# Turning attention keys on VectorE and through DRAM, and a new row order for the layer-norm tiles

## The chip, the core and the metric

The kernel runs on one core of one Trainium2 chip, as one launch. The time is device time in microseconds, from the runs of the whole program. A run with the profiler on gives the trace; its span runs from the first to the last recorded instruction. The engines are called here as the profile calls them: PE (TensorE: matrix products and transposes), DVE (VectorE), ACT (ScalarE), POOL (GpSimd) and SP (SyncE, which here only issues DMAs). Each engine works through its own list of instructions in order and waits on semaphores where an operand is not ready.

## What is computed

The input x is 2 sequences of 1024 tokens with 512 features, in float32. Four blocks follow, each added to its own input:

```
x = x + attn_a(layernorm(x))    # chunked linear attention with decay, 4 heads of 128
x = x + ffn(layernorm(x))       # gated, weights are integer codes with scales, 1408 hidden
x = x + attn_b(layernorm(x))    # softmax attention, one head of 512
x = x + ffn(layernorm(x))       # the same weights again
```

The change is mostly in the first block. For each chunk of 128 tokens and each head it computes

```
k      = k / max(norm(k), 1e-12)
attn   = (q @ k.T) * beta * decay          # causal
y      = attn @ v + (q @ state) * chunk_decay
state  = state * total_decay + v.T @ (k * beta * decay_to_end)
```

The product q @ k.T needs the key with its 128 features across the partitions (its transpose), while the state needs it with the tokens across the partitions. So every key tile is needed in both layouts.

## The kernel before

**Tiles.** Rows of x are cut in 16 tiles of 128 tokens (NT = 16), and these in 4 groups of ST = 4 tiles (NST = 4). Between the blocks x lies in DRAM, one DRAM tile for each row tile (x1, x2, x3, lines 139 to 141). Most products are made in three passes of a high and a low part (`mm3`, line 88), which `split` (line 73) makes: ACT copies the high part, DVE or POOL subtracts it to get the low one.

**Layer norm in groups.** `ln_norm` (line 188) loads a row tile, normalizes it, and turns it on DVE into a staging tile y. DVE turns blocks of 32 by 32 only, so the blocks have still to be put in place: `ln_move` (line 201) does that by DMAs from SBUF to SBUF, four for each of four blocks b, that is 16 of 64 KB for a group. There are 14 such groups in all, with 224 moves: the profile has 152 on SP and 72 on POOL. Row tile i of group st is the 128 rows in a line from row 512 st + 128 i, so a move writes 16 runs of 32 values (128 bytes) on each partition. `ln_split` (line 214) or `combine` (line 242) then make high and low parts. The first two groups of the first block are turned on PE instead (`layernorm_T`, line 125).

**The first attention's loop** (lines 749 to 804) takes one tile in each step t. It emits, in this order: one query head of four steps ahead (`q_head`, line 500: 12 products of 512 columns), the key and value of tile t + 1 (`kv_tile`, line 577), the scores of tile t (`scores`, line 617), every fourth step the gate projection of a coming group (`gate_proj`, line 426), the decay of tile t + 1 (`decay`, line 528), and fillers: layer-norm steps of later groups by the table at line 733, weight codes (`down_weights`, line 304) and, in the last three steps, operands and products of the block that follows. `scores(t)` begins with

```
            pkT = psum(f"pkT{t}").rearrange("p (h c) -> p h c", h=H)
            for h in range(H):
                nc.tensor.transpose(pkT[:, h, :], kf[:, h, :], ident)
            kT = tl("kT", t)
            copied = nc.scalar.copy(kT, pkT).ins
```

(lines 620 to 624): PE turns the key of each of the four heads into PSUM, and ACT copies it to SBUF as kT. Then come the state's products (pd, line 635), the outputs of the tile before (`chunk_out`, line 660: pl, pg), and the scores proper (pS, line 650), which read kT as the stationary operand. DVE weighs pS by decay into the tile at (line 654). The key itself is taken from PSUM to SBUF as sWk by DVE (line 571) one step earlier, in `kv_part` (line 558), and its squared norms are made on ACT (`k_norm`, line 581).

**Order.** The tile framework takes the program's order as priorities, and settles each engine's list before the run by a model of the times; `behind` (line 66) adds an order among instructions of one engine. At the table of line 733 the first four entries of a group are its four `ln_norm` steps, the last four its four `ln_move` steps; the number is the loop step in which each is emitted. Groups 2 and 3 of the first block are split at steps 3 and 7 (line 771), one step before their first query head. Row tiles of x1 are written by `chunk_out(t)`, which `scores(t + 1)` calls.

**What follows.** After the loop comes `spill` (line 177) of a product V to DRAM, by way of tiles that take the place of sq, kT, kw and sdec. `ffn` (line 808) does the gated block with 11 hidden tiles twice, the second attention follows, and `ffn` again. Both call `ln_steps` (line 225) for their layer norms.

## Time and profile before

| what | value |
|---|---|
| median of 3 runs | 927.32 us (926.01 to 927.61) |
| the profiled execution | 926.9 us |
| its span | 925.2 us, granted PE clock 1.00 |
| instructions | 13659 |
| busy: PE, DVE, ACT, POOL | 918.5, 690.4, 433.9, 257.4 us |
| DMA packets | 216182, of these under 512 bytes 151024 |
| DMA bytes | 162.20 MB, mean 175 GB/s |

How to read it: busy time is the time in which an engine had at least one instruction running, so instructions that overlap count once. A group's mean is the length of one instruction, and where instructions are pipelined the distance from start to start is shorter than that. "Idle before" is the time in which an engine stood still ahead of an instruction, with what ended the wait. In rows of slices each digit is a fortieth of the span (23.1 us), in tenths. DMA rows give the size and the median time from issue to landing; SPq is SP's queue of instructions.

The stages of the run, from the lines at work on PE: preparation to 49 us, the first attention's loop to about 231, the first gated block to 455, the second attention (its first products from 442) to 701, the last gated block to the end.

### The profile page before, as it was taken

Reading aid. Unit: us, or ns where it says so; the run is one execution under the profiler, and the core shown is the slowest. Engines: PE = TensorE matmul, PEld = TensorE weight load, DVE = VectorE, ACT = ScalarE, POOL = GpSimd, SP = SyncE. Lnnn points to the kernel's source line nnn. Section 1 sums busy time; section 2 is a strip of 40 time slices with the busy share of each in tenths; the row PEclk is TensorE's granted clock in tenths of the full one; section 3 lists DMA queues with packets and bytes.
Section 4 is the critical chain, followed back from the end, with each engine's and each line's share of the span. In section 5 each row is a group of like instructions: output and inputs, shape, how many; then the busy total and the mean of one; then the engine's idle time right before and its main releaser. Section 6 shows DMA issues by size and latency. Waiting matters only on the chain.

```text
span 925.2 us, 13659 instructions
## 1 busy us (share of the span) xinstructions
PE 918.5 (99%) x4546; PEld 778.1 (84%) x4546; DVE 690.4 (75%) x1335; ACT 433.9 (47%) x928; POOL 257.4 (28%) x458
## 2 busy tenths in 40 slices
PE   9999999999999999999999999999999999999998
PEld 7899999998888888888888888888878888888887
DVE  6755657479998798778848878569968886967654
ACT  5645365556776334444234444145434444344431
POOL 4345334557563002211130401140501631001100
PEclk9999999999999999999999999999999999999999
DMA  9535655477979754724733769225969735454022
GB/s 304 210 100 124 208 160 152 158 207 262 367 236 321 214 178 153 216 47 150 281 82 83 171 168 261 69 45 137 239 140 369 259 126 137 165 205 138 22 69 80
DMA packets 216182, 162.20 MB, mean 175 GB/s; under 512 B 151024, under 2 KB 167728, under 8 KB 216112
## 3 DMA queue, kind: packets, MB, share of 16 engines
q1 hardware_dynamic: 212624, 150.05, 53.7%
q0 software_dynamic: 3488, 11.28, 4.5%
q8 instruction: 36, 0.59, 0.3%
q14 instruction: 34, 0.28, 0.1%
HBM read 104.76 MB, written 41.84 MB: 158 GB/s over the span
## 4 chain that ended last, share of the span: by engine, by line
PE 94%; DVE 2%; SPq 1%; DMA 1%; issue 1%; ACT 0%; POOL 0%; DVEq 0%; ACTq 0%
PE pXf L338 4%; PE pog L925 4%; PE pog L924 4%; PE pZf L338 4%; PE pof L925 4%; PE pXg L338 4%; PE pVg L338 4%; PE pVf L338 4%; PE pZg L338 4%; PE pof L924 4%; PE pob L91 3%; PE pob L89 3%; PE pob L90 3%; PE psZ L1023 2%; PE psX L1023 2%; PE psV L1023 2%
## 5 line engine op out<-in xcount | busy, mean ns | idle before, releaser
L924 PE MATMUL pog<-wdg,hsg 128*128 128x512 f32 (+1 forms) x165 | 60.1, 375 | 0.0
L925 PE MATMUL pog<-wdg,hsg 128*128 128x512 f32 (+1 forms) x165 | 60.0, 375 | 0.0
L925 PE MATMUL pof<-wdf,hsf 128*128 128x512 f32 x154 | 59.1, 389 | 0.0
L924 PE MATMUL pof<-wdf,hsf 128*128 128x512 f32 x154 | 58.9, 389 | 0.0
L91 PE MATMUL pob<-vh,ptl 128*128 128x512 f32 x128 | 49.9, 390 | 0.8 <-DVE ptl L76 0.8
L89 PE MATMUL pob<-vh,pth 128*128 128x512 f32 x128 | 49.9, 390 | 0.0
L90 PE MATMUL pob<-vl,pth 128*128 128x512 f32 x128 | 49.8, 389 | 0.0
L76 POOL TENSOR_TENSOR hsg<-sgg,hsg 128x128 fp32r<-128x128 f32 x40 | 18.9, 491 | 110.4 <-ACT hsg L75 102.6
L338 PE MATMUL pXg<-B_g,wcg 128*128 128x512 f32 x176 | 46.2, 389 | 0.0
L338 PE MATMUL pVf<-T_f,wcf 128*128 128x512 f32 x176 | 46.2, 389 | 0.0
L338 PE MATMUL pVg<-T_g,wcg 128*128 128x512 f32 x176 | 46.2, 389 | 0.0
L338 PE MATMUL pXf<-B_f,wcf 128*128 128x512 f32 x176 | 45.9, 390 | 0.0
L113 POOL TENSOR_SCALAR ve_g<-mv_g 128x1 f32<-128x1 f32 x16 | 7.7, 486 | 129.6 <-DVE mv_g L111 129.6
L209 POOL DMA_DIRECT2D xT_g<-y_g x48 | 31.1, 655 | 38.5 <-DVE T_b L76 29.2
L338 PEld LDWEIGHTS pXf<-B_f,wcf 128*128 128x128 f32 x176 | 32.9, 188 | 7.1 <-issue 0.3
L338 PEld LDWEIGHTS pVf<-T_f,wcf 128*128 128x128 f32 x176 | 33.0, 188 | 6.9
L338 PEld LDWEIGHTS pVg<-T_g,wcg 128*128 128x128 f32 x176 | 33.0, 188 | 6.9
L338 PEld LDWEIGHTS pXg<-B_g,wcg 128*128 128x128 f32 x176 | 33.0, 188 | 6.9
L545 ACT ACTIVATE row<-row,ncl 128x128 f32<-128x128 f32 x64 | 20.5, 391 | 35.4 <-POOL row L534 35.4
L113 POOL TENSOR_SCALAR ve_b<-mv_b 128x1 f32<-128x1 f32 x16 | 5.7, 359 | 112.4 <-DVE mv_b L111 112.2
L924 PEld LDWEIGHTS pog<-wdg,hsg 128*128 128x128 f32 x165 | 31.1, 188 | 5.7
L925 PEld LDWEIGHTS pog<-wdg,hsg 128*128 128x128 f32 x165 | 31.0, 188 | 5.6
(344 smaller groups left out, 2837.4 us busy)
## 6 DMA issues: line engine op xcount, KB each, us to landing
wcg<-wc SPq DMA_DIRECT2D x19, 896.0 KB, 5.0
wc<-wcf SPq DMA_DIRECT2D x11, 896.0 KB, 5.8
p<-py SPq DMA_DIRECT2D x15, 512.0 KB, 3.5
wcf<-wc SPq DMA_DIRECT2D x8, 896.0 KB, 6.3
ptl<-p SPq DMA_DIRECT2D x56, 128.0 KB, 3.1
xin_a<-in_x SPq DMA_DIRECT2D x16, 256.0 KB, 5.3
xra<-in_x SPq DMA_DIRECT2D x16, 256.0 KB, 3.4
row<-cl SPq DMA_DIRECT2D x16, 256.0 KB, 4.3
```

The source lines that it names most:

```text
L76: return c.ins, (eng or nc.vector).tensor_tensor(lo, src, hi.bitcast(F32), ALU.subtract).ins
L89: nc.tensor.matmul(ps, lhs_hi, rhs_hi, start=first, stop=False)
L90: nc.tensor.matmul(ps, lhs_hi, rhs_lo, start=False, stop=False)
L91: end = nc.tensor.matmul(ps, lhs_lo, rhs_hi, start=False, stop=last).ins
L113: nc.gpsimd.tensor_scalar(ve, mv[:, 1:2], EPS, None, ALU.add)
L209: (nc.sync if sync else nc.gpsimd).dma_start(out=xf[32 * b : 32 * (b + 1), :, c, :], in_=y[32 * c : 32 * (c + 1), b].rearrange("p k i q -> ...
L338: nc.tensor.matmul(ps, w[:, m, k * P : (k + 1) * P], o[:, s, k, :], start=first and k == 0 and s == 0, stop=k == 1 and s == 1, skip_group_ ...
L545: nc.scalar.activation(row[:, h, :], row[:, h, :], AF.Exp, bias=ncl[:, n : n + 1], scale=-1.0)
L924: nc.tensor.matmul(ps, hs[i][0][:, j], wd[j][:, ds], start=j == 0, stop=False)
L925: nc.tensor.matmul(ps, hs[i][1][:, j], wd[j][:, ds], start=False, stop=j == KH - 1)
L1023: ends[nm] = nc.tensor.matmul(ps, o[:, i, k], w[:, j, k], start=first and k == 0 and i + j == 0, stop=k == 1 and i == 1, skip_group_check= ...
```

## The change

Three things change.

1. **Keys.** `scores` no longer turns the key on PE. The new function `turn_key`, which `kv_tile` calls between the key and the value of a tile, turns all four heads on DVE in blocks of 32 by 32 (tile ky), writes the result to a DRAM tile k_d (256 KB) and reads it back by four DMAs (64 KB each, in pieces of 128 bytes) to kT, all on SP. `key_copy`, which other steps are put behind, now holds the DVE instruction in place of the ACT copy, and `k_norm` of the next tile is put behind nothing. The tiles sq and ky have one buffer each; sq had two. The V spill uses the buffers of at in place of sq.
2. **Row order in a layer-norm tile.** DRAM tiles of x1, x2 and x3 now hold a whole group (512 rows). Tile i of a group takes 32 rows of each quarter of the group, in place of 128 rows in a line. After DVE's turn a move then writes 4 runs of 128 values (512 bytes) on each partition, in place of 16 runs of 32. The number of moves and their bytes are the same. Since a tile takes rows of all four row tiles, its load waits until all four are written.
3. **Order of the steps.** The table that places the layer-norm steps in the loop of the first attention has new numbers.

The diff, cut to its core (what is left out gives the functions below groups in place of row tiles):

```diff
+    def in_tiles(groups):
+        return [x[i * P : (i + 1) * P, :] for x in groups for i in range(ST)]
+
-    x1 = [dp.tile([P, D], F32, tag=f"x1_{t}", name=f"x1_{t}") for t in range(NT)]
...
+    x1_g = [dp.tile([ST * P, D], F32, tag=f"x1_{g}", name=f"x1_{g}") for g in range(NST)]
+    x1 = in_tiles(x1_g)
...
+    k_d = [dp.tile([P, 4, P], F32, tag=f"k_{t}", name=f"k_{t}") for t in range(NT)]
...
             if (nm, n) not in lnX:
-                lnX[nm, n] = load_x(src[n], f"{nm}{n}")
+                rows = src[st].rearrange("(c i q) d -> i c q d", c=4, i=ST)
+                lnX[nm, n] = load_x(rows[n - st * ST], f"{nm}{n}")
...
-        xf = lnT[nm, st].bitcast(F32).rearrange("p k (i b q) -> p (k i) b q", i=ST, b=4)
+        xf = lnT[nm, st].bitcast(F32)
...
-                out=xf[32 * b : 32 * (b + 1), :, c, :],
-                in_=y[32 * c : 32 * (c + 1), b].rearrange("p k i q -> p (k i) q"),
+                out=xf[32 * b : 32 * (b + 1), :, c * P : (c + 1) * P],
+                in_=y[32 * c : 32 * (c + 1), b].rearrange("p k i q -> p k (i q)"),
...
+        def turn_key(t):
+            y = tl("ky", t, pool=a1)
+            turned = nc.vector.transpose(
+                y.rearrange("p h c -> p (h c)"), kva[t][0].rearrange("p h c -> p (h c)")
+            ).ins
+            key_copy[:] = [turned]
+            nc.sync.dma_start(out=k_d[t], in_=y)
+            kTa[t] = kT = tl("kT", t)
+            placed = k_d[t].rearrange("(c q) h (b j) -> b q h c j", c=4, b=4)
+            for b in range(4):
+                nc.sync.dma_start(
+                    out=kT[32 * b : 32 * (b + 1)].rearrange("p h (c j) -> p h c j", c=4), in_=placed[b]
+                )
+
         def kv_tile(t):
             kv_part(t, "Wk")
+            turn_key(t)
             kv_part(t, "Wv")
...
-            sq = tl("sq", t)
+            sq = tl("sq", t, pool=a1)
...
-            pkT = psum(f"pkT{t}").rearrange("p (h c) -> p h c", h=H)
-            for h in range(H):
-                nc.tensor.transpose(pkT[:, h, :], kf[:, h, :], ident)
-            kT = tl("kT", t)
-            copied = nc.scalar.copy(kT, pkT).ins
-            key_copy[:] = [copied]
+            kT = kTa.pop(t)
             if t == 0:
-                with behind((copied,)):
+                with behind(key_copy):
                     decay(0)
             if t + 1 < NT:
-                k_norm(t + 1, copied)
+                k_norm(t + 1)
...
-            (xa, "a", 2, (0, 0, 0, 1, 1, 1, 1, 1)),
-            (xa, "a", 3, (2, 2, 3, 4, 4, 5, 5, 5)),
-            (x1, "f", 0, (6, 6, 7, 7, 7, 7, 8, 8)),
-            (x1, "f", 1, (9, 9, 10, 10, 10, 10, 11, 11)),
+            (x_g, "a", 2, (0, 0, 0, 1, 1, 1, 2, 2)),
+            (x_g, "a", 3, (3, 3, 4, 4, 5, 5, 6, 6)),
+            (x1_g, "f", 0, (7, 7, 7, 7, 8, 8, 9, 9)),
+            (x1_g, "f", 1, (10, 10, 10, 10, 11, 11, 11, 11)),
...
-        spilled = spill(ap, ("sq", "kT", "kw", "sdec"), next(prep)[0], vo_d, "V")
+        spilled = spill(ap, ("at", "kT", "kw", "sdec"), next(prep)[0], vo_d, "V")
```

More of the change, by code (lines that the diff above doesn't have):

```diff
@@ L136, in hybrid_block_kernel @@
     bq_s, sg_s, su_s = cols[:, 0:H], cols[:, H : H + KH], cols[:, H + KH : H + 2 * KH]
+    def in_tiles(groups):
+        return [x[i * P : (i + 1) * P, :] for x in groups for i in range(ST)]
     x_in = a["x"]
-    x1 = [dp.tile([P, D], F32, tag=f"x1_{t}", name=f"x1_{t}") for t in range(NT)]
-    x2 = [dp.tile([P, D], F32, tag=f"x2_{t}", name=f"x2_{t}") for t in range(NT)]
-    x3 = [dp.tile([P, D], F32, tag=f"x3_{t}", name=f"x3_{t}") for t in range(NT)]
+    x1_g = [dp.tile([ST * P, D], F32, tag=f"x1_{g}", name=f"x1_{g}") for g in range(NST)]
+    x1 = in_tiles(x1_g)
+    x2_g = [dp.tile([ST * P, D], F32, tag=f"x2_{g}", name=f"x2_{g}") for g in range(NST)]
+    x2 = in_tiles(x2_g)
+    x3_g = [dp.tile([ST * P, D], F32, tag=f"x3_{g}", name=f"x3_{g}") for g in range(NST)]
+    x3 = in_tiles(x3_g)
     cl_d = [dp.tile([16, P], F32, tag=f"cl_{g}", name=f"cl_{g}") for g in range(NST)]
+    k_d = [dp.tile([P, 4, P], F32, tag=f"k_{t}", name=f"k_{t}") for t in range(NT)]
     p_d = [dp.tile([T // P, P, P], F32, tag=f"p_{i}", name=f"p_{i}") for i in range(NC)]
@@ L367, in hybrid_block_kernel @@
         normed, key_copy, late_norm = {}, [], []
-        xTa, za, gta, sca, qTa, kva, ata, deca, sta, rowa, facta = ({} for _ in range(11))
+        xTa, za, gta, sca, qTa, kva, ata, deca, sta, rowa, facta, kTa = ({} for _ in range(12))
         wqkv = {}
@@ L410, in load_wqkv @@
             return load if staged is None else done
-        xa = [x_in[t * P : (t + 1) * P, :] for t in range(NT)]
+        x_g = [x_in[g * ST * P : (g + 1) * ST * P, :] for g in range(NST)]
+        xa = in_tiles(x_g)
         def ln_tile(t):
@@ L916, in ffn @@
                     with behind((half,)):
-                        nc.sync.dma_start(out=xr, in_=src[t])
+                        nc.sync.dma_start(out=xr, in_=in_tiles(src)[t])
                     o = fp.tile([P, 512], F32, tag="sg", name=f"o{nm}{t}")
@@ L940, in hybrid_block_kernel @@
     ffn(
-        x1,
+        x1_g,
         x2,
@@ L946, in hybrid_block_kernel @@
         spilled,
-        (ln_steps(x2, "b", 0) + ln_steps(x2, "b", 1), of_b[:6]),
+        (ln_steps(x2_g, "b", 0) + ln_steps(x2_g, "b", 1), of_b[:6]),
     )
@@ L1201, in hybrid_block_kernel @@
         for b in range(NB):
-            nm, src, g = ("b", x2, 2) if b == 0 else ("g", x3, 0)
+            nm, src, g = ("b", x2_g, 2) if b == 0 else ("g", x3_g, 0)
             norm = ln_steps(src, nm, g) + ln_steps(src, nm, g + 1)
@@ L1277, in hybrid_block_kernel @@
     out_t = [out[t * P : (t + 1) * P, :] for t in range(NT)]
-    ffn(x3, out_t, "g", wcs, moving, ended, ([], []))
+    ffn(x3_g, out_t, "g", wcs, moving, ended, ([], []))
 def _layouts(i):
```

## The prediction

> **What bounds the kernel now.** I began with the page's busy shares, its slices and its chain of work.

> ```profile
> PE 918.5 (99%) x4546; PEld 778.1 (84%) x4546; DVE 690.4 (75%) x1335; ACT 433.9 (47%) x928; POOL 257.4 (28%) x458
> ...
> DVE  6755657479998798778848878569968886967654
> ...
> PEclk9999999999999999999999999999999999999999
> ...
> PE 94%; DVE 2%; SPq 1%; DMA 1%; issue 1%; ACT 0%; POOL 0%; DVEq 0%; ACTq 0%
> ```

> PE (TensorE) is busy 918.5 of 925.2 us at the full granted clock, and 94% of the chain is its own work. Whatever leaves PE is gained one for one, unless a wait takes its place. VectorE (DVE) is full in slices 10 to 12 (208 to 278 us). Next I asked for the tile that the change takes away, pkT, and for TensorE in order of time about it.

> ```profile
> L622 PEld LDWEIGHTS pkT<-ident,sWk x64: 138/141/144, 49.2 to 217.6; 128*128 128x128 f32 x64
> L622 PE MATMUL pkT<-ident,sWk x64: 270/273/274, 49.3 to 217.7; 128*128 128x128 f32 x64
> L624 ACT COPY kT<-pkT x16: 562/585/588, 50.0 to 221.0; 128x512 f32<-128x512 f32 x16
> ...
>   PE pS L650: 0.4, 1
> ```

> ```profile
> 49.19 0.28 PE L91 MATMUL pWv<-Wv,xl_a 128*128 128x256 f32 x1
> 49.31 0.60 PE L622 MATMUL pkT<-ident,sWk 128*128 128x128 f32 x4
> 49.75 0.61 PE L635 MATMUL pd<-sWv,kw 128*128 128x128 f32 x4
> ```

> The 273 ns of one transpose overlap the next. What counts is start to start: four take 49.75 - 49.31 = 0.44 us, and the matmul before them takes 0.12 whatever follows. The other tiles show the same step (64.36 to 64.79, 163.57 to 164.01).

> **The keys, on PE and ScalarE.** 16 tiles x 0.44 us leave PE: **-7.0 us**. The single PE wait for this copy goes too (0.40 us ahead of 100.59): **-0.4**. 16 copies of 0.585 us leave ScalarE, which is 56% busy between 49 and 222 us; that shortens nothing on the path.

> **The keys, the new way.** Each tile now takes one VectorE transpose of 128x512, one write of 256 KB on SyncE's queue (SP) and, once that has landed, four reads of 64 KB in pieces of 128 bytes. The nearest rows:

> ```profile
> L198 DVE STREAM_TRANSPOSE y_a<-xn_a x8: 670/711/714, 60.1 to 108.6; 128x512 f32<-128x512 f32 x8
> ```

> ```profile
> x<-xra SPq DMA_DIRECT2D x16, 256.0 KB, 2.3
> ...
> xT_a<-y_a SPq DMA_DIRECT2D x32, 64.0 KB, 2.1
> ```

> ```profile
> L1116 SPq DMA_DIRECT2D ptl<-p x56: 303/600/2538, 502.7 to 675.5; - x56
> ...
> DMA to landing us min/median/max: 2.1/3.1/5.0
> ```

> The first is the same VectorE form; x<-xra has the write's size; ptl<-p, in the second attention, is the same write-then-four-reads pattern at twice the size. From the moment VectorE begins to take the key out of PSUM: 0.68 (that row, L571) + 0.70 + 2.3 + three issues of 0.60 ahead of the last read + 3.1 = **8.6 us**. The reads lie between ptl's 3.1 and xT_a's 2.1; I take the longer.

> The room for it is the time from the start of sWk (L571) to the first pS (L650) of the same tile, less 0.44 for the transposes that go. By the trace, for tiles 0 to 15: 9.3, 18.1, 12.6, 15.0, 15.5, 19.9, 12.0, 13.8, 13.4, 19.1, 14.4, 14.9, 10.5, 12.1, 10.2, 10.6. The key is made a loop step before its scores, so all 16 have room; the shortest margins are 0.7 (tile 0), 1.6 (tile 14), 1.9 (tile 12) and 2.0 us (tile 15). In an in-order queue a late key is paid in full: pS waits on PE, and behind it stand the gate projection or the next query head. Bounds: nothing, and 21.5 us if both legs take their worst (worked out under the rivals). I take **+0.5**, since only tile 0 lies within a microsecond, and other PE work may be planned ahead of it.

> **VectorE.** 16 x 0.70 = 11.2 us are added to an engine that is 64% busy between 49 and 222 us. Its idle time hides that until about 197 us. From there I read it in 8 us stretches (the columns are PE, PEld, VectorE, ScalarE, GpSimd, each busy and count, then clock, DMA share, GB/s):

> ```profile
> 197.00:205.00 8.00, 8.00 (x61) 7.50 (x60) 6.87 (x14) 3.10 (x13) 4.26 (x7) 1.00 0.68 182
> 205.00:213.00 8.00, 8.00 (x61) 7.50 (x60) 6.93 (x14) 6.29 (x14) 5.24 (x7) 1.00 1.04 390
> 213.00:221.00 8.00, 8.00 (x45) 6.86 (x45) 8.00 (x18) 7.17 (x18) 4.31 (x6) 1.00 0.64 217
> 221.00:229.00 8.00, 8.00 (x53) 7.15 (x53) 6.75 (x14) 3.86 (x7) 7.84 (x8) 1.00 0.51 192
> 229.00:237.00 8.00, 8.00 (x37) 6.59 (x36) 7.96 (x15) 4.66 (x8) 4.66 (x8) 1.00 0.89 357
> 237.00:245.00 8.00, 8.00 (x37) 6.64 (x36) 7.42 (x13) 7.07 (x10) 4.87 (x9) 1.00 1.00 333
> ```

> VectorE is busy 43.9 of these 48 us: 4.1 us idle. Two more transposes (tiles 14 and 15) take 1.4 of that, and PE arrives earlier by three sets of transposes, 1.3 us. So 1.4 us stays idle and the cover just holds on average; if none of the idle time can be used, PE waits 2.7 us. Bounds 0 and 2.7; I take **+1.0**, nearer to nothing, because in 213 to 221 VectorE is full and PE still does not wait.

> **SP.** Per tile 0.33 + 4 x 0.60 = 2.7 us of issue are added, and the first read stands behind the landing of its write (2.3 us), with everything later on that queue behind it: the rows of decays (row<-cl), residuals (xra) and layer-norm moves. What waits for those is VectorE and ScalarE, not PE; their cover is the room above and PE's next 8 to 10 us. Loss: inside the 0.5.

> **Layer-norm moves.** Instead of 16 runs of 128 bytes per partition, each of the 224 moves now has 4 of 512. On SP an xT_a move takes 0.63 us and 16 of them 11.9 us (75.42 to 87.33); the write p<-py, which has 512-byte pieces, issues in 0.37 us. So some 0.25 us of SP time per move goes, 16 us over the 64 moves issued in the first attention. No PE instruction waits for a move there, so I cost it at **0** (bounds: -0.4, which is already counted, and +1 if a split comes late).

> [...]

> **Spread and row choice.** The moves of groups 2 and 3 go one or two steps later; they must precede the splits at steps 3 and 7, and the last move now falls in step 2 and step 6. A layer-norm tile now needs four earlier row tiles instead of one, but the first such step (7 for x1 tiles 0 to 3) comes three steps after the last of them is written. The squares get one buffer, and only ScalarE writes them. The V spill takes the "at" buffers, free after L668 at 228.9 us, while the product ends at 231.5. All at 0.

> **Sum.** The profiled execution took 926.9 us (span 925.2): 926.9 - 7.0 - 0.4 + 0.5 + 1.0 = **921.0**. The median of the runs shown is 0.4 above it: **921.4**.

> **Rivals.** *Chance 0.62: the forecast*, 918.5 to 923.5.

> *Chance 0.15: VectorE or the keys take half back.* VectorE's whole 2.7 and a chain of 10.6 us (late by 1.3, 0.1 and 0.4 at tiles 0, 12 and 14): 926.9 - 7.4 + 2.7 + 1.8 = 924.0, or 924.4. For it speaks the full stretch at 213; against it, that PE waits for VectorE only 1.3 us in the whole run.

> *Chance 0.12: no change that shows.* A chain of 11.0 us (1.7, 0.5, 0.8, 0.4 late) and the 2.7: 925.6, or 926.0; also the case that the new order of instructions spoils as much as it frees. A measurement of this kernel tells about 0.2% (1.9 us) from no change.

> *Chance 0.11: slower.* One mechanism: both DRAM legs take as long as these rows at their worst, 5.8 us for the write (the longest x<-xra) and 5.0 for a read, as the first attention's queue is shared with weight and code loads. The chain is then 0.68 + 0.70 + 5.8 + 1.8 + 5.0 = 14.0 us, and tiles 0, 2, 6, 7, 8, 12, 13, 14, 15 are late by 4.7, 1.4, 2.0, 0.2, 0.6, 3.5, 1.9, 3.8, 3.4: 21.5 us, at most 926.9 - 7.4 + 21.5 = 941.0. It decides from a chain of 12.0 us, where tiles 0, 12, 14, 15 lose 7.4 together. For it: DMA shares of 0.6 to 1.0 in the stretches above; against it: the medians, and 86 thousand fewer small pieces (224 moves x 384).

> **Numbers.** 921.4 is the likeliest case. The range 918.0 to 927.5 leaves out most of the slower case and a little below. Faster 0.77, same 0.12, slower 0.11.

> **What would show it.** pkT gone and PE's instruction count down by 64; PE's wait list naming kT or ky on DMA if the keys are late (tile 0 at about 50 us first, then 190 to 225); VectorE waits on PE's list between 195 and 245 if that cover fails; moves at about 0.37 us on SP; packets under 512 bytes well down from 151 thousand. A stall of PE above 3 us between 45 and 225 would make the forecast wrong.

## The result, and the profile after

| | before | after |
|---|---|---|
| median, same chip | 927.47 us (926.01 to 928.0) | 1026.03 us (1021.21 to 1028.5) |
| ratio, 95% interval | | 1.1059 [1.1015, 1.1104] |
| profiled span | 925.2 us | 1026.8 us |
| PE busy / idle in the span | 918.5 / 6.7 us | 942.3 / 84.5 us |
| PE instructions | 4546 | 4482 |
| DMA packets, of these under 512 bytes | 216182, 151024 | 193239, 106576 |

The change made the kernel slower by a tenth; the forecast was 921.4 us, and its range ended at 927.5. These are the lines of the page after that answer to those shown of before: busy shares, clock, chain, and the group of VectorE's statistics on the layer-norm tiles f (columns of a group: busy time and mean ns, then idle time just before it and what ended it).

```profile
PE 942.3 (92%) x4482; PEld 789.1 (77%) x4482; DVE 699.6 (68%) x1351; ACT 425.4 (41%) x912; POOL 241.9 (24%) x458
...
PEclk9998999897889999999999899989999999999999
...
PE 51%; DMA 27%; DVE 8%; SPq 5%; issue 3%; POOL 3%; ACT 2%; DVEq 0%; ACTq 0%; POOLq 0%
...
L109 DVE BATCH_NORM_STATS2 bn_f<-xin_f 128x6 f32<-128x512 f32 x16 | 11.0, 692 | 52.3 <-DMA xin_f<-x 52.2
```

Three things are to be seen. PE fell from 94% of the chain to 51%, and DMAs rose from 1% to 27%: the kernel is no longer bound by one engine but by hand-overs. VectorE stands 52.2 us for the loads xin_f, where it stood 14.5 us before; this wait belongs mostly to the row choice and not to the keys (it is 37.2 us with the rows alone and 17.7 with the keys alone, two kernels of the next section). And although PE does 64 instructions less, it is busy 23.8 us longer, with a granted clock under 1.0 in several slices.

The list of PE's waits (total, times, longest) names late tiles. Of the names used from here on, kw is the key times its factors s (made by POOL, the operand of the state's product), sq the key's squares from which s is made (ScalarE), sWv the value, and xh_a and xT_a are the high and low parts of a layer-norm group.

```profile
PE pd L657 <- POOL kw L639: 14.9, 3, 10.6
PE pS L672 <- issue: 11.9, 1, 11.9
...
PE pS L672 <- DMA kT<-k: 9.4, 5, 3.2
```

The longest wait for kw, 10.6 us at 225 us, stands behind a load: VectorE waits 8.71 us for xin_f before it updates the state, and POOL's list waits 8.29 us for that state with kw behind it. Only 9.4 us are put down to a key that lands late. The 11.9 us "issue" is a key too: the timeline of SP shows the four reads of one key on both sides of a run of 16 layer-norm moves (start, length, line, tile).

```profile
245.25 1.25 SPq L599 DMA_DIRECT2D kT<-k  x2
246.55 10.28 SPq L219 DMA_DIRECT2D xT_f<-y_f  x16
256.88 1.28 SPq L599 DMA_DIRECT2D kT<-k  x2
```

The moves of 512 bytes take 10.28 us for 16 here; one move's issue fell from 627 to 599 ns (median of xT_f), and not to the 370 that the prediction hoped for. The time is lost in the stages where VectorE takes layer-norm tiles of x:

| PE reaches | before, us | after, us | this stage grew by |
|---|---|---|---|
| the first gated block (first pXf) | 227.1 | 289.7 | 62.6 |
| last pof | 455.0 | 524.4 | 6.8 |
| end of the second attention (last pob) | 701.0 | 795.1 | 24.7 |
| end of the span | 925.2 | 1026.8 | 7.5 |

The keys are used in the first attention alone, so they are hardly the whole cause: of the 39 us after it, the keys alone lose 1.1 (699.2 us from the first pXf on, 698.1 before).

### The profile page after: what moved, and what is told of

Its sections match the earlier page's. It is cut to its first block, busy times and chain, and to the rows that moved or that the text cites. A ratio compares the mean times of both kernels' runs of the same rounds, so it can differ in the third digit from the quotient of the medians.

```text
span 1026.8 us, 13674 instructions
## 1 busy us (share of the span) xinstructions
PE 942.3 (92%) x4482; PEld 789.1 (77%) x4482; DVE 699.6 (68%) x1351; ACT 425.4 (41%) x912; POOL 241.9 (24%) x458
## 2 busy tenths in 40 slices
DMA packets 193239, 170.59 MB, mean 166 GB/s; under 512 B 106576, under 2 KB 142736, under 8 KB 193168
## 4 chain that ended last, share of the span: by engine, by line
PE 51%; DMA 27%; DVE 8%; SPq 5%; issue 3%; POOL 3%; ACT 2%; DVEq 0%; ACTq 0%; POOLq 0%
DMA xin_f<-x 6%; PE pog L947 4%; PE pog L946 4%; PE pof L947 3%; PE pof L946 3%; PE pXg L348 3%; DMA xin_a<-in_x 3%; PE pVg L348 3%; DMA xin_g<-x 3%; DMA xin_b<-x 3%; PE pZg L348 3%; PE pob L91 2%; PE pob L89 2%; PE pob L90 2%; PE pVf L348 2%
## 5 line engine op out<-in xcount | busy, mean ns | idle before, releaser
L91 PE MATMUL pob<-vh,ptl 128*128 128x512 f32 x128 | 51.2, 400 | 5.5 <-DVE ptl L76 5.5
L109 DVE BATCH_NORM_STATS2 bn_f<-xin_f 128x6 f32<-128x512 f32 x16 | 11.0, 692 | 52.3 <-DMA xin_f<-x 52.2
L672 PE MATMUL pS<-qT,kT 128*128 128x128 f32 x128 | 20.9, 316 | 21.2 <-issue 11.9
L672 PEld LDWEIGHTS pS<-qT,kT 128*128 128x128 f32 x128 | 18.8, 226 | 22.4 <-issue 18.8
L113 POOL TENSOR_SCALAR ve_b<-mv_b 128x1 f32<-128x1 f32 x16 | 3.5, 228 | 136.9 <-DVE mv_b L111 136.8
## 6 DMA issues: line engine op xcount, KB each, us to landing
xin_a<-in_x SPq DMA_DIRECT2D x16, 256.0 KB
xra<-in_x SPq DMA_DIRECT2D x16, 256.0 KB
k<-ky SPq DMA_DIRECT2D x16, 256.0 KB
```

The lines of the kernel that those rows point to most:

```text
L91: end = nc.tensor.matmul(ps, lhs_lo, rhs_hi, start=False, stop=last).ins
L109: nc.vector.bn_stats(bn, xin)
L113: nc.gpsimd.tensor_scalar(ve, mv[:, 1:2], EPS, None, ALU.add)
L672: nc.tensor.matmul(pS[:, h, :], kT[:, h, :], qTa[st][:, h, bass.ts(i, P)], start=True, stop=True)
```

## The experiments

The theories were, in the words of the expectations: **A**, a load of a layer-norm tile in the new row order runs on about four of the 16 DMA engines; **B**, the keys' way through DRAM; within it **C**, runs of 16 moves on SP stand ahead of a key's DMAs, and **D**, the chain of turn, write and reads is too long by itself; **E**, POOL, given the moves, is late with its own work. Each time below is a median, with its ratio to the kernel before on the same chip.

### The two parts, each alone

*Keys alone* keeps turn_key and takes back row order and table (x still lies in DRAM in groups, one DRAM tile for each). *Rows alone* keeps the row order, and the keys go through PE:

```diff
 # keys alone
-                rows = src[st].rearrange("(c i q) d -> i c q d", c=4, i=ST)
-                lnX[nm, n] = load_x(rows[n - st * ST], f"{nm}{n}")
+                lnX[nm, n] = load_x(in_tiles(src)[n], f"{nm}{n}")
...
 # rows alone
-            turn_key(t)
...
+            for h in range(H):
+                nc.tensor.transpose(pkT[:, h, :], kf[:, h, :], ident)
```

> The keys by VectorE and DRAM alone; the row order, the loads and moves of the layer-norm tiles and the table of steps as before the change. Theory A (the row loads of the layer-norm tiles, whose outer dimension is 4, run on about 4 of 16 DMA engines: 4.2 busy on average between 173.5 and 176 us after the change; they come late, and POOL, ACT, SP and at last PE wait behind them): this kernel is near the one before, 919 to 932 us, with PE waits for kT under 5 us in all. Theory B (the keys' way through DRAM is what is late): most of the 99 us stay in the first attention's loop, 970 us or more.

Measured: 951.94 us, 1.0264 [1.0243, 1.0285]: between the ranges of the two theories.

> The row order alone (loads of 32 rows of each quarter, moves with 512-byte pieces); the keys turned by PE and the table of steps as before the change. Theory A: most of the loss is here, 975 to 1030 us, with VectorE's waits for xin_a and xin_f at several times the 18 us of before. Theory B: only what the later blocks lost (about 7 + 25 + 8 us by the stages of the two traces), 930 to 970 us, and the first attention's loop within 5 us of the 186 us before.

Measured: 988.02 us, 1.0635 [1.0602, 1.0668]. Each part loses, the rows more: 24.7 and 60.8 us beside the 98.6 of both. With the rows alone PE reaches the first pXf at 259.3 us (32 late), and the second attention, which has no such keys, takes 20 us longer: the waits of PE for opS (8.6 us) and ptl (5.5 us) there, 10.9 and 5.5 in the whole change, belong to the rows.

### Rows: how many DMA engines a load runs on

In the whole change the timeline of VectorE and that of PE have this place (idle time just before, and what ended it, in brackets):

```profile
178.19 0.69 DVE L109 BATCH_NORM_STATS2 bn_f<-xin_f 128x6 f32<-128x512 f32 x1 [8.98 <-DMA xin_f<-x]
```

```profile
179.86 0.39 PE L89 MATMUL pc<-wc,xh_a 128*128 128x264 f32 x1 [2.50 <-DVE sWv L582]
```

Two loads xin_f were issued at 171.02. VectorE waits 8.98 us for the first; the key's turn and sWv are behind it in its list, and PE waits for sWv. The table by stretches shows what the DMA engines do at that time (the last three columns are clock, DMA share, GB/s):

```profile
178.00:179.50 1.50, 0.00 (x0) 0.00 (x0) 1.31 (x3) 0.00 (x0) 0.00 (x0) 1.00 0.26 100
```

All packets of this stretch are of about 2048 bytes, the size of the loads' rows. The DMA share is 0.26, that is 4.2 of 16 engines, at 100 GB/s: at this rate 256 KB take 2.6 us, and two loads, one behind the other, 5.2. The source of this load has an outermost dimension of 4 (`[4, 32, 512]`: quarters, rows, columns). Two kernels change this alone. *Four loads* issues each quarter as a DMA of 32 rows of its own; *sixteen* lets a tile take 8 rows of each sixteenth of a group, so that the outermost dimension is 16, with the staging tile y ordered to suit, and moves that still write 512 bytes:

```diff
 # rows alone, four loads
-                lnX[nm, n] = load_x(rows[n - st * ST], f"{nm}{n}")
...
+                for c in range(4):
+                    nc.sync.dma_start(out=xin[32 * c : 32 * (c + 1), :], in_=rows[n - st * ST, c])
...
 # rows alone, sixteen
-                rows = src[st].rearrange("(c i q) d -> i c q d", c=4, i=ST)
+                rows = src[st].rearrange("(c i q) d -> i c q d", c=16, i=ST)
```

> As the row order alone, but each layer-norm load is cut in four DMAs of 32 rows, one for each quarter, so that each can run on all DMA engines; SP issues three more DMAs per tile. Theory A: the loss goes, 925 to 945 us (what is left is 56 x 3 more issues on SP). Theory B says nothing on it beyond: the same as the row order alone.

Measured: 940.74 us, 1.015 [1.0119, 1.0182].

> The row order alone, with 8 rows of each sixteenth of a group in a tile in place of 32 rows of each quarter: the same number of loads, bytes and move pieces (512 bytes), but a load whose outer dimension is 16; the blocks are put in place by the layout that VectorE's turn writes to. Keys by PE, table as before the change. Theory A (a load runs on as many DMA engines as its outer dimension has): the loss of the row order goes, 924 to 934 us, and VectorE's waits for xin fall to what they were (18 us for xin_a and xin_f). If instead the strided rows or the 512-byte moves are what costs, it stays at 980 us or more.

Measured: 931.30 us, 1.0048 [1.0031, 1.0065]. The group of VectorE's statistics, in rows alone and then in sixteen:

```profile
L109 DVE BATCH_NORM_STATS2 bn_f<-xin_f 128x6 f32<-128x512 f32 x16 | 11.0, 693 | 37.2 <-DMA xin_f<-x 37.2
```

```profile
L109 DVE BATCH_NORM_STATS2 bn_f<-xin_f 128x6 f32<-128x512 f32 x16 | 10.9, 688 | 16.5 <-DMA xin_f<-x 16.5
```

The wait goes from 37.2 to 16.5 (14.5 before), PE's idle time to 9.2 us, and of the 60.8 us above the kernel before 4.5 are left. Everything else of the row order is still there: every load waits for four row tiles, and its issue takes as long (0.54 us where the kernel before has 0.32). So theory A holds for these two shapes: the share of the DMA engines was 0.26 with 4, and in sixteen, after two such loads issued at 175.07, it was 0.90 from 176.5 to 178 us and 0.94 from 178 to 179 (268 and 272 GB/s, with a load of codes beside them from 176.35). Four loads get most of it back; on how many engines each of the four ran is not shown. They cost SP four issues each, but what their other 9 us are is not shown: the longest later wait, 6.2 us of VectorE for xin_g at 742 us, stands behind a run of 8 such loads that spreads over 10.42 us of SP's list, of which 3.1 us are issues; SP itself waits there for loads of weights (wcg).

The same two mends in the whole change:

> The whole change, with each layer-norm load cut in four DMAs of 32 rows. Theory A: near the keys alone, 920 to 945 us. Theory B: the loop of the first attention stays slow, 975 us or more. If part of the loss comes from reads of one key standing on both sides of a run of moves in SP's list (two kT reads at 245.25, sixteen moves, two reads at 256.88 after the change), it lies between, and the wait is seen on pS.

Measured: 960.94 us, 1.0369 [1.0336, 1.0403], between the two ranges.

> The whole change with the loads mended as in the kernel with eight rows of each sixteenth, and nothing else altered. If the loads are the whole of the row part, the time is that of the keys alone plus the 4.5 us of the mended rows: 951.9 + 4.5 = 956 us (952 to 961), and the waits for xin_f on VectorE's list fall from 52 us to under 20. If the row part has a second cost that only shows beside the keys (the two parts alone sum to 85.5 us of the 98.8), it is 965 to 970 us.

Measured: 959.26 us, 1.0341 [1.0316, 1.0367]. So 66.8 of the 98.6 us are the loads (1026.03 - 959.26), and 7.3 us are left for the new row order and the table beside the keys (959.26 - 951.94). The whole was 13 us above the sum of its parts (98.6 against 85.5); with the loads mended 3 us of these are left (32.2 against 24.7 + 4.5). That late loads and late keys add up because they share the lists of SP and VectorE is an argument, not a measurement. The waits for xin_f fall from 52.2 to 22.9 us, not under 20 as expected, and two long stalls of PE stay: 10.9 us for a key whose reads stand on both sides of 16 moves, and 8.3 us for kw behind a load that VectorE awaits for 6.90 us.

### Keys: what is late

With keys alone, one wait stands out on PE:

```profile
PE pS L671 <- DMA kT<-k: 20.8, 6, 8.0
```

The longest but one is that of tile 3. VectorE turned its key from 77.13 to 77.84; SP's timeline about it goes (and PE's after it):

```profile
76.54 11.47 SPq L218 DMA_DIRECT2D xT_a<-y_a  x16
88.11 0.56 SPq L594 DMA_DIRECT2D k<-ky  x1
...
90.50 2.63 SPq L598 DMA_DIRECT2D kT<-k  x4
```

```profile
94.98 2.04 PE L671 MATMUL pS<-qT,kT 128*128 128x128 f32 x8 [7.31 <-DMA kT<-k]
```

The write goes out 10 us after the turn, behind a run of 16 moves. That is theory C, and the next kernels take the moves off SP (a, and f of groups 0 and 1: those of the loop), or make the run short, or take the keys off SP:

```diff
 # moves on POOL
-            sync = nm in "af" or ...
+            sync = nm == "a" and False or (nm == "f" and st > 1) or ...
 # moves on ACT
-            (nc.sync if sync else nc.gpsimd).dma_start(
+            (nc.scalar if nm == "a" or (nm == "f" and st < 2) else nc.sync if sync else nc.gpsimd).dma_start(
 # moves on POOL, kw on VectorE
-            weighted = nc.gpsimd.tensor_tensor(kw, kf, ...)
+            weighted = nc.vector.tensor_tensor(kw, kf, ...)
 # one move: one plain DMA of 1 MB per loop group in place of 16 moves
 # keys on ACT
-            nc.sync.dma_start(out=k_d[t], in_=y)
+            nc.scalar.dma_start(out=k_d[t], in_=y)      # and the four reads
```

> The keys alone (row order and table as before the change), with the layer-norm moves of the first attention's loop issued by POOL in place of SP. Theory C (a key is late because its write or its reads stand in SP's list behind a run of 8 to 16 moves, 7 to 11.5 us of issue: in the keys alone the write of key 3 leaves at 88.1 behind moves from 76.5, that of key 12 at 209.5 behind moves from 201.6): PE's waits for kT fall from 20.8 us to under 6 and the time to 920 to 935 us. Rival D (the landings of the chain itself are too long, whatever stands before them): the waits stay at 15 us or more, 945 us or more. Rival E: POOL, which makes kw and the decay rows, becomes late by its moves; then PE waits for kw or at instead.

Measured: 951.85 us, 1.027 [1.0253, 1.0287]. The waits for kT fell from 20.8 to 1.4 us, as theory C had it, and the time did not move: PE waits 20.2 us for kw, POOL's product, in its place, as theory E had it: POOL issues the 16 moves from 76.27 to 87.40 and ends kw of tile 3 at 93.67.

> The keys alone, with the loop's moves issued from ACT's list. SP is as free as with the moves on POOL, and POOL's list as without. Theory C with E (POOL's list held kw back when it issued the moves): waits for kT and for kw both under 6 us; 920 to 938 us, if ACT, which has 75 us idle in the loop, can bear some 40 us of issue. If ACT becomes late, the waits are for qT, the decay row or the high parts, and the time is 940 us or more.

Measured: 953.53 us, 1.0291 [1.0273, 1.0309]. Waits: kw 16.1, kT 6.6, la 3.8 us. POOL issues no moves here, but now ScalarE does: its 16 moves fill its list from 76.78 to 89.99, the squares sq behind them start at 90.09, and kw, which needs them, is late again (9.9 us).

> The keys alone, moves of the loop on POOL as in the run before, and the product kw made by VectorE in place of POOL. Theories C and E: the 20 us of waits for kw go, 922 to 935 us, and what is left stands behind VectorE. If POOL's moves hold back more than kw (the decay rows, the factors s), then at or kw still come late and the time is 940 us or more.

Measured: 968.79 us, 1.0451 [1.0434, 1.0468]. kw is late from VectorE too: 30.8 us in 4 waits. In the longest, 15.0 us up to 99.48, VectorE stands 4.67 us for the factor s, which POOL still makes, behind its moves (78.08 to 88.64) and a wait of 3.77 us for a decay row. So theory E holds in its wider form, which this expectation names: moves on POOL hold back all that POOL makes. The three kernels agree: in whichever list the run of 16 moves stands, what that engine does next is late, the key's DMAs on SP, s and kw on POOL, sq on ScalarE.

> The keys alone, and in the loop of the first attention one plain DMA of 1 MB on SP per layer-norm group in place of its 16 moves (groups 2 and 3 of the first block, 0 and 1 of the second): the same bytes, but the values land in the wrong places, so that part is left uncomputed. Theory C (runs of moves on SP hold up the keys' DMAs): PE's waits for kT stay under 5 us with POOL's list as in the keys alone, 918 to 930 us. Rival D (the chain of two DMAs is too long by itself): 940 us or more.

Measured: 943.02 us, 1.0175 [1.016, 1.019]. (In this kernel the values of those groups are not put in place.) Waits for kT: 11.6 us. So the runs of moves are worth 9 us of the 25; the rest needs no run. Its longest stall, 9.0 us up to 211.28, comes at a place where the DMA engines are full (share 0.98 to 1.09 from 196 to 208 us, 345 to 434 GB/s): the key's write lands 7.4 us after its issue at 195.07, and SP issues the reads only at 205.03.

> The whole change with both mended: loads of 8 rows of each sixteenth, and the moves of the first attention's loop on POOL. If theories A and C are all there is, the 7 us of transposes come through: 917 to 930 us. If the two parts cost anything else together, more than 930.

Measured: 960.19 us, 1.036 [1.0344, 1.0375], with PE waiting for kw (9.3), xh_a (5.9), kT (4.5), sWv (4.2) and others: no gain on the 959.26 of the same kernel with its moves on SP.

> The keys' part alone, with the write and the four reads of each key issued from ScalarE's list in place of SP's; SP's list is that of the kernel before. The key no longer stands behind a run of 16 moves. Theory C (runs of moves on SP hold the keys back) expects PE's waits for kT to fall under 3 us and the time to be 922 to 930 us if nothing else becomes late. Theory D (the chain itself is too long) expects the waits for kT to stay near 20 us and 950 us. Since ScalarE's list now stands still for the landing of each write (2.0 to 2.8 us, sixteen times), a wait of PE for what ScalarE makes (decays, the high parts, query heads) may take the place: 940 to 955 us.

Measured: 943.68 us, 1.0182 [1.0165, 1.0199]. Waits for kT 8.2 and for its write 2.1, xh_a 3.1. Neither C (under 3 us of such waits) nor D (near 20) has it. 8 us go when the keys leave SP's list; since ScalarE's list now stands for the writes, as the third case of the expectation had it, what SP's part would be by itself is not shown.

Two more kernels changed the reads. One reads with a single plain DMA, the other reads the key of the tile before, which should have landed:

```diff
 # one read
-            for b in range(4):
-                nc.sync.dma_start(out=kT[32 * b : 32 * (b + 1)]..., in_=placed[b])
+            nc.sync.dma_start(out=kT, in_=k_d[t])
 # earlier key
-            placed = k_d[t].rearrange(...)
+            placed = k_d[max(t - 1, 0)].rearrange(...)
```

> The keys' part alone, with one plain read of 256 KB per key in place of four reads of 64 KB in pieces of 128 bytes: the blocks of 32 by 32 come back where they were and not in place, so this part of the computation is left out. SP's list still stands for the landing of each write before the read. What goes is three issues of a read for each of 16 keys, some 35 us of the 146 us that SP spends issuing in the loop of the keys alone (88 us in the kernel before), and 30 thousand small packets. If SP's fullness is the price of the way through DRAM, the time falls from 952 to 933 to 940 us. If it is the latency of write, wait and read on the key's own way, PE's waits for kT stay near 20 us and the time at 945 to 952 us.

Measured: 943.15 us, 1.0166 [1.013, 1.0202], waits for kT 14.1 us: between the two. SP's issuing in the loop, the sum of its DMA instructions from 49 us to the first pXf, fell to 95 of 193 us: it is 82 of 178 us in the kernel before, 138 of 203 with keys alone, 85 of 192 with the keys on ACT. (The 146 and 88 us of the expectation take in the gaps within a row of the timeline.)

> The keys' part alone, but the four reads of tile t take the DRAM tile of t - 1 (which landed a step earlier): the scores use the key of the tile before, so this part of the computation is wrong by one tile. All DMAs, their sizes and their places in SP's list stay, and VectorE's turns too; only SP's wait for the landing of the write just issued goes, which took 20.7 us of SP's time in the keys alone (8 waits in its list of waits). If SP's standing still is the price of the way through DRAM, the time falls from 952 to the 932 to 937 us of the kernel with the turn but no DMAs. If it is the issue time (2.7 us a tile) and the traffic of the five DMAs behind the runs of moves, it stays at 945 to 952 us, with PE waiting for kT on the same two tiles (about 95 and 216 us, 7 to 8 us each).

Measured: 953.02 us, 1.0272 [1.024, 1.0304]. The run did not do what it was made for: SP still stood 15.9 us for writes (20.7 before), and the order of its list changed: the reads of one key stand on both sides of the next key's write at 91.01. But it shows one thing. Waits for kT fell to 1.5 us and the time stayed; qT (6.6 us) and kw (6.6) are late in place of it. The tile that PE's list names is not by itself what the time hangs on.

### Keys: is the wait direct, and is there a gain at all

Four kernels separate the gain from the price. *Both ways* is the kernel before, with its PE transposes, and beside them the whole new path, whose result nothing reads; in the second of the kind the reads land in DRAM. *Turn alone* is keys alone without DMAs; *no turn* gives the scores the untransposed key.

```diff
 # both ways, on the kernel before
+            turn_key(t)                 # lands in ky (second kernel: in a DRAM tile)
...
 # turn alone
-            y = tl("ky", t, pool=a1)
-            nc.sync.dma_start(out=k_d[t], in_=y)       # and the four reads
+            kTa[t] = kT = tl("kT", t)                   # VectorE turns into kT
...
 # no turn
+            kTa[t] = kva[t][0]
```

> The kernel before, with its PE transposes and the ScalarE copy, and beside them the whole new path of the keys: VectorE's turn of 0.70 us, the write of 256 KB, and the four reads of 64 KB, which land in a tile that nothing reads. No score waits for the new path. If a late kT at pS is what the keys cost (theories C and D: a direct wait), PE has nothing new to wait for and the time is 927 to 932 us. If the cost is what the five DMAs and the turn do to the lists of SP and VectorE (other loads and moves stand behind a write that has to land), it stays at 940 us or above, and PE's wait list names other tiles than kT.

Measured: 950.37 us, 1.0254 [1.0234, 1.0274].

> As the kernel with both ways, but the four reads of a key land in DRAM in place of VectorE's tile ky, so that the next turn waits for the write alone, as in the change, and not for the reads. If the 23 us of the kernel with both ways came of VectorE's turn waiting for the reads to land (6.5 us once at 216 us), it falls to 930 to 938 us. If they come of SP's list standing still for each write, it stays at 943 to 951 us, with PE waiting for at, xh_a or qT and not for a key.

Measured: 954.65 us, 1.0297 [1.0282, 1.0312], a little above the second case. No score waits for a DMA in these two, and they cost 23 and 28 us (VectorE's turn, 6 us by the ladder below, is in both). So the price of the way through DRAM is largely indirect, and not an artefact of the shared tile. Three lines of the first one's waits on PE, then one link of such a chain on VectorE and on ScalarE:

```profile
PE pq L89 <- ACT xh_a L75: 5.6, 1, 5.6
PE pl L684 <- DVE at L670: 3.9, 1, 3.9
PE pS L666 <- ACT kT L640: 3.3, 4, 1.3
```

```profile
144.70 0.69 DVE L109 BATCH_NORM_STATS2 bn_f<-xin_f 128x6 f32<-128x512 f32 x1 [5.59 <-DMA xin_f<-x]
```

```profile
146.08 0.31 ACT L604 ACTIVATE sq<-sWk 128x128 f32<-128x128 f32 x1 [5.79 <-DVE mv_f L111]
```

SP issues a key's write at 133.66, its reads only at 136.88, when the write has landed, and the two loads xin_f behind them at 141.57 and 142.57 (132.71 and 134.08 in the kernel before). VectorE's list stands 5.59 us for the load, ScalarE's 5.79 us for VectorE's mean, the high part xh_a is late, and PE stands 5.57 us at 147.92 for a query head. No key is in this chain but on SP.

> The keys' part alone, with VectorE's turn written directly into kT and no DMA for the keys at all: the blocks of 32 by 32 are not put in place, so this part of the computation is left out. PE loses its 64 transposes and ScalarE its 16 copies; VectorE has 16 turns more. By the prediction's first and third terms (-7.4 and +1.0) it takes 926.9 - 6.4 = 920.5 us, between 919 and 922. If VectorE's cover is what fails, it stands above 927 us and PE waits for VectorE between 190 and 245 us. If it is near 920, the whole 24.7 us of the keys alone, and the 7 that did not show, are the price of the way through DRAM.

Measured: 931.96 us, 1.0056 [1.0039, 1.0074], where the forecast's terms gave 920.5.

> The keys are not turned at all: the scores read the untransposed key sWk as their stationary operand, so this part of the computation is left out. PE loses its 64 transposes and ScalarE its 16 copies, and VectorE, SP and the DMA engines get nothing new. If the 7.4 us of the prediction's first terms are there to be had, it takes 926.9 - 7.4 = 919.5 us (918 to 921), and the 5 us by which the kernel with VectorE's turn stood above the kernel before are the price of sixteen turns of 0.70 us on VectorE's list. If it stays at 924 us or above, the gain itself does not come: with fewer instructions the lists of all engines are settled anew, and PE waits in other places for what it no longer does itself.

Measured: 925.76 us, 0.9989 [0.9976, 1.0001]. Even with the transposes gone, and nothing put in their place, the kernel gains 1.2 us and not 7.4; the interval just reaches no change. It keeps the smaller things that came with the keys (DRAM tiles of x by groups, one buffer of sq, k_norm behind nothing, the V spill through at), and no run takes these out by themselves: what they cost, if anything, is in the 1.2 too. The page and the waits of this kernel:

```profile
PE 912.4 (99%) x4482; PEld 771.4 (84%) x4482; DVE 689.6 (75%) x1335; ACT 426.5 (46%) x912; POOL 256.3 (28%) x458
```

```profile
PE pq L90 <- DVE xT_a L76: 2.4, 1, 2.4
PE pr L505 <- ACT qT L529: 1.4, 1, 1.4
...
PE pd L648 <- POOL kw L630: 0.5, 1, 0.5
```

PE's busy time did fall, by 6.1 us, but its idle time rose by 4.2 (6.7 to 10.9): PE now stands for what VectorE, ScalarE and POOL make, at places where it did not stand before. The 2.4 us stand at 140 us: VectorE's list has two statistics steps ahead of the low part xT_a, and both wait for loads (1.22 and 0.94 us).

## Why the prediction was wrong

The steps between the kernels make a ladder, each rung one term of the sum:

| rung | median, us | step | the prediction had |
|---|---|---|---|
| before (926.8 to 927.5 on the chips used) | 927.0 | | |
| keys not turned at all | 925.8 | -1.2 | -7.4 |
| VectorE turns them, no DMA | 932.0 | +6.2 | +1.0 |
| and they go through DRAM on SP | 951.9 | +20.0 | +0.5 |
| and new row order and table, loads on 16 engines | 959.3 | +7.3 | 0 |
| loads as in the change | 1026.0 | +66.8 | 0 |

The rungs hold in this order: without the keys the loads cost 56.7 us (988.02 - 931.30).

**The step that failed most is "Layer-norm moves ... I cost it at 0", with the row choice "All at 0".** It priced the moves, which get larger pieces, and of the loads only that they wait for four row tiles. It never looked at the shape that the row choice gives the load itself: same bytes, same 2048-byte pieces, but an outermost dimension of 4. The runs showed 66.8 us for that, and 4.5 us for the row order without it (rows alone, sixteen). The gain it did name, 16 us of SP time by issues of 0.37 us, did not come: 599 ns in place of 627.

**"SP ... Loss: inside the 0.5" failed next**, with the +0.5 itself. It found the right places (rooms of 9 to 20 us, and "everything later on that queue behind it") but counted a tile's 2.7 us of issue without summing them over the queue. In the loop SP issued 82 of 178 us before and 138 of 203 with the keys, and there stood 19.1 us for keys' writes to land: a queue half full became one with over three quarters of its time taken (157 of 203 us), where a run of 16 moves (11.5 us) ahead of a write is longer than any margin. And what waits behind SP was said to be "VectorE and ScalarE, not PE", with cover; both ways shows that this cover does not hold (5.6 us on PE through a load, VectorE and ScalarE).

**The slower rival** named one mechanism, both legs at their worst. Legs of 5.8 and 5.0 us were the exception: in keys alone the longest write took 5.9 us and the longest read 5.6, but the medians were 2.7 and 2.6. What made the chain long was the time ahead of them in SP's list, 10 us for tile 3 (77.84 to 88.11), which no row of a landing time contains. The 86 thousand fewer small pieces that were held against it are 44 thousand on the page: the keys' reads bring 34 thousand of their own (151024 to 185072 with keys alone).

**-7.0 and -0.4.** The transposes left as predicted (64 instructions, 6.1 us of busy time), but "whatever leaves PE is gained one for one, unless a wait takes its place" had the wrong weight: in the profiled runs waits took 4.2 us of it, and the median shows 1.2. That PE was 99% busy did not mean that the others had room; by these waits, they came just in time.

**VectorE, +1.0** (bounds 0 and 2.7) measured +6.2; the profiled spans, 923.3 and 930.7, differ by 7.4. Half of these, 3.7, are lost in the loop (the first pXf comes at 225.2 and at 228.9), and part of them where the prediction looked: in turn alone VectorE has no idle time between 210 and 225 us, and PE loses 1.5 us there (1.0 for the low part of V, and the end of a wait for kw that no turn has too, 0.5 us at 208); with no turn PE is busy for all of these 15 us.

```profile
210.00:225.00 15.00, 13.54 (x87) 11.96 (x88) 15.00 (x29) 11.30 (x28) 8.02 (x10) 1.00 0.69 241
```

Another part is the clock: the stall for xT_a, 2.42 us with no turn, is 2.56 us here, and after it PE works 3.4 us at half clock (0.50 from 142 to 144 us), which it does not with no turn (1.00 from 138 to 146). The other 3.7 us come after the loop, where no key is left: between 243 and 294 us PE waits four times for what VectorE and ScalarE make for the first gated block (sgf, pZf, T_f; 2.8 us together), and not once with no turn. Whether that is work which the full stretch pushed back, or the new order into which the lists are settled when instructions are added, these runs do not separate.

**The clock.** The prediction had no term for it. PE did the same 4482 instructions in 912.4 us busy with no turn and in 942.3 after: 29.9 us more. 47.4 us of this busy time lie in stretches at half clock, and that accounts for 23.7 of them; the rest is not shown. The stretches of keys alone after its stall at tile 3 show how it comes (columns as before, PE busy first, third from the end the clock):

```profile
94.00:96.00 2.00, 1.02 (x5) 1.05 (x6) 2.00 (x4) 0.00 (x0) 0.16 (x1) 0.50 0.69 209
96.00:98.00 2.00, 2.00 (x8) 1.81 (x8) 2.00 (x8) 0.00 (x0) 0.00 (x0) 0.50 0.78 231
98.00:100.00 2.00, 2.00 (x7) 1.53 (x7) 1.42 (x5) 0.49 (x2) 0.99 (x3) 0.64 1.09 239
100.00:102.00 2.00, 2.00 (x11) 1.65 (x10) 0.00 (x0) 2.00 (x5) 0.74 (x2) 1.00 0.91 219
```

After 7.3 us of standing still PE works at half clock until about 99 us: products of 512 columns follow each other in 0.43 us in place of 0.23, and the stall costs some 2 us more than its own length (4 us of work at half speed). The whole 101.6 us of the span are idle time on PE (+77.8) and this longer busy time (+29.9), less the transposes (-6.1). "A stall of PE above 3 us between 45 and 225 would make the forecast wrong" was a good sign to watch, but its window was too narrow for the kernel it was to judge: in the change one stall of 3.3 us falls in it (at 77 us, for kw), and the long ones, 10.6 and 11.9 us, begin at 225 and 249, where the loop had slipped to. Keys alone has three in it (7.3, 3.1 and 8.0 us).

**What stays open.** Of the 20 us of the way through DRAM, about 9 go with the runs of moves (one move), about 9 with three of the four reads (one read) and about 8 with SP's list (keys on ACT). These overlap and do not add up to a bill, and no kernel here took SP's standing for the write away by itself. No list was found that bears the runs of moves beside the keys; no version that computes the whole beat the kernel before.

## What to carry to other kernels

When an edit changes which rows a DMA takes, look at the pattern of that DMA and not only at its bytes and pieces: 56 loads of unchanged size cost 67 us here because their outermost dimension went from 128 to 4. Before adding DMAs to an in-order queue, sum what it issues and waits for over the whole stage, and look for the longest run ahead of a time-critical one; moved to another engine's list, the run delays what that engine makes. An engine that is 99% busy does not promise its time back: take the work out alone, with nothing in its place, and measure what that is worth before a replacement is built.
